# Epsilon as the bias of ScalarE's root, combiner products in quadrants and modulation rows in column tiles, in the attention stage of a two-layer adaLN kernel

## The chip, the cores and the metric

The kernel runs on one core of one Trainium2 chip. Its time is the device time of one execution, in microseconds (us); several executions give a median. Besides, one execution was recorded by the hardware profiler, and every duration and start below comes from it. The engines of the core are TensorE (PE in the profile, with PEld for its weight loads), VectorE (DVE), ScalarE (ACT) and GpSimd (POOL); SyncE (SP) issues most of the DMAs.

## The reference, cut to what matters

`x` has 4 batches of 1,024 tokens with 256 features, all in float32. There are two layers. Each takes six modulation rows per batch from a small condition, and normalises twice. Cut to layer 0, with layer 1 in a line:

```python
mod = (silu(c) @ wmod).reshape(B, 6, 1, D)          # sa, ca, ga, sb, cb, gb
ga = (2 * (ga >= 0) - 1) * maximum(abs(ga), 0.25)   # and gb
h = layernorm(x) * (1 + ca) + sa                    # (x - mean) / sqrt(var + 1e-5)
x = x + ga * linear_attention(h, queries, combiners)
h = layernorm(x) * (1 + cb) + sb
x = x + gb * experts(h)                             # 8 experts, top 2, 256 -> 1024 -> 256, relu
# layer 1: the same frame with a gated MLP that decays chunk by chunk, and 8 experts, top 2
```

The attention has no softmax. With `x` cut into slices of 64 features, it comes down to a Gram matrix of each slice over all tokens, a product of it with the combiners, and a product of that with the queries, which gives one matrix `md` per batch that all its tokens are multiplied by.

## The kernel before, in words

**Stages.** The first 104 us are the attention stage: loads, modulation rows, normalisation, attention, second normalisation, routing to experts. At its end the routed tokens are listed by expert in blocks of 128 and gathered from a table in memory, `h_rows`. Then the expert blocks run to 592 us, one after the other (`p_h`, L1610, is a block's first product, `p_y`, L1634, its second), and then layer 1, to 1073 us. The three edits of the change lie in the attention stage, with one DMA in the blocks.

**What sets the order there.** The stage is a list of pieces given to `Plan` (L47). Each piece has an engine, a cost in us, the pieces it comes after, the buffers it holds, a rank and perhaps an earliest time. `Plan.run` is a list scheduler: it plays the pieces through by their costs, lower ranks first, and emits the instructions in the order that this gives on every engine. On the chip each engine then works through its own list in that order and waits where an operand isn't there. So a changed cost or rank changes the order of instructions, not only of the piece it belongs to.

**A batch, first half** (`first_half`, L1220; `FIRSTS` holds the ranks of the four batches). `normalised` (L1085) takes groups of four chunks of 128 tokens: per chunk `bn_stats` and `bn_aggr` on DVE (L1097, L1098) into `ln_mv`; after the fourth chunk, `ln_v` = variance + epsilon (L1101); a square root on ScalarE (L1105); a Newton step for the reciprocal root on DVE, five small instructions (`newton`, L1109 to L1116); then the scaled tokens `xn` by GpSimd or ScalarE (L1126, L1128). `to_features` transposes them on TensorE (`pm_t`, L1168) and applies shift and scale on ScalarE (`h1T`, L1173); `to_tokens` transposes back (`pm_b`, L1195) and copies (L1200). TensorE takes the Gram matrices of the 64-feature slices (`pm_gram`, L1256); DVE copies them into the diagonal of a block-diagonal tile `gd` (L1267); `head_t1` (L1286) multiplies by the combiners, two products of 256 columns (`pm_t1`, shown as `pm_t` by the profile at L1289); ScalarE copies that to `t` (L1299); `pm_m` (L1311) multiplies by the queries; DVE gates it into `md` (L1324).

**A batch, second half** (`second_half`, ranks in `SECONDS`). For each pair of chunks TensorE multiplies by `md` (`pm_o`, L1352) and DVE adds to `x` (L1362). A second normalisation follows by the same `normalised`, then features again (`h2T`), the router's logits (`pm_e`, L194; `le`, L1395; `pm_l`, L1404), the choice of two experts on DVE (`route`, L420 to L446, thirteen instructions), and the way back to tokens. SP stores a group's tokens (`h_rows<-xn`, L1449, 512 KB) and, after each routing, the marks of who was chosen (`h_rows<-g_meta`, L1436). The last batch in the order, number 3, is routed in two groups (`SPLIT`).

**The handover.** When all is routed, products over the tokens give each token's place (`pm_turn`, L454 on; `g_pairs`, L466), the bounds of the first blocks (`g_limit`, L603; `g_reached`, L817), and counts (`pm_counts`, L847), from which DVE finds the row numbers of blocks 0 and 1 (L860, L869). GpSimd gathers the rows (`fetch`, L353), TensorE transposes them (`pm_x`, L1562), ScalarE copies them (L1674), and `p_h` begins.

**Modulation rows of layer 1.** Beside this, `modulation_rows` (L1512) computes layer 1's six rows: three pairs, each of four matmuls that stream 256 columns for 4 output rows (`pm_mod`, L1523), and per row one copy by ScalarE (`modulation1`, L344 on; L348 adds one to a scale row, L350 copies). They land side by side on four partitions of `half1`. In the blocks, two of them are turned into gates on DVE, and one DMA writes all to memory (L2173). Small filler products (`pm_busy`, L1033) keep TensorE running.

Of the kernel before, what the change touches and what calls it, by code (L numbers as in the profile page):

```python
# [8 lines left out]
F32 = mybir.dt.float32  # L9
F16 = mybir.dt.float16  # L10
I32 = mybir.dt.int32
AF = mybir.ActivationFunctionType
ALU = mybir.AluOpType
# [6 lines left out]
P = 128  # L20
B, S, D = 4, 1024, 256
NC = S // P
KD = D // P
# [4 lines left out]
EPS = 1e-5  # L28
# [117 lines left out]
def adaln_d2_kernel(  # L146
# [20 lines left out]
    nc = tc.nc  # L167

    const = ctx.enter_context(tc.tile_pool(name="const", bufs=1))
# [5 lines left out]
    ps_2 = ctx.enter_context(tc.tile_pool(name="ps_2", bufs=2, space=PSUM))  # L175
    ps_m = ctx.enter_context(tc.tile_pool(name="ps_m", bufs=3, space=PSUM))

    def psum(pool, shape, name):
        tag = {id(ps_1): "p1", id(ps_2): "p2", id(ps_m): "pm"}[id(pool)]
        t = pool.tile([P, 512], F32, tag=tag, name=name)  # L180
        n = 1
        for s in shape[1:]:
            n *= s
        v = t[: shape[0], :n]
        if len(shape) == 3:
            v = v.rearrange("p (a b) -> p a b", b=shape[2])
        return v
# [21 lines left out]
    rw_sb = const.tile([P, KD, STRIP], F32, name="rw_sb")  # L209
    br_sb = const.tile([P, 1], F32, name="br_sb")  # L210
    half1 = pw.tile([P, W1ROW], F32, name="half1")
    rows1 = half1[:B, : 6 * D].rearrange("p (i d) -> p i d", d=D)
    gb0 = const.tile([P, B, D], F32, name="gb0")
    poolA = tc.tile_pool(name="poolA", bufs=2)
    pa = poolA.__enter__()
    qT = pa.tile([P, KD, 4, 64], F32, name="qT", bufs=1)
    comb = pa.tile([P, KD, 4, 64], F32, name="comb", bufs=1)
# [20 lines left out]
    for b in range(B):  # L238
        for g in range(2):
            cs = slice(4 * g, 4 * g + 4)  # L240
# [21 lines left out]
    ones = const.tile([P, P], F32, name="ones")  # L262
    nc.gpsimd.memset(ones, 1.0)
    rank = const.tile([P, E], F32, name="rank")
# [50 lines left out]
    def silu_of(layer, cT):  # L315
        sT = pa.tile([P, KD, ROUTER], F32, name=f"sT{layer}", bufs=1)
        nc.vector.memset(sT, 0.0)
        nc.scalar.activation(sT[:, :, :B], cT, AF.Silu)
        return sT
# [21 lines left out]
        nc.vector.tensor_scalar(size, size, 0.25, None, ALU.max)  # L341
        nc.vector.scalar_tensor_tensor(dst, sign, -1.0, size, ALU.add, ALU.mult)

    def modulation1(pr, piece, i):  # L344

        dst, src = rows1[:, 2 * piece + i, :], pr[:, i * D : (i + 1) * D]
        if (2 * piece + i) % 3 == 1:
            nc.scalar.activation(dst, src, AF.Identity, bias=ones[:B, :1])  # L348
        else:
            nc.scalar.copy(dst, src)  # L350

# [665 lines left out]
    for k in range(KD):  # L1017
        nc.sync.dma_start(h_rows[B * S :, k * P : (k + 1) * P], ones[:1, :])
    nc.sync.dma_start(h_rows[B * S :, D:], g0.beyond[:1, :])
    sT0 = silu_of(0, c0)  # L1020
    sT1 = silu_of(1, c1)
    gate_rows = pa.tile([B, 2, D], F32, name="gate_rows", bufs=1)
# [4 lines left out]
    tiles = {}  # L1027
# [61 lines left out]
    def normalised(b, cs, key, slot, after, rank, at=0.0):  # L1089

        n = len(cs)

        def stats(c):
            if c == cs[0]:
                tiles["mv", key] = pa.tile([P, n, 2], F32, tag="ln_mv", name="ln_mv", bufs=6)
            st = pa.tile([P, 6], F32, tag="ln_st", name="ln_st", bufs=4)
            nc.vector.bn_stats(st, x_sb[:, c, b, :])  # L1097
            nc.vector.bn_aggr(tiles["mv", key][:, c - cs[0], :], st)  # L1098
            if c == cs[-1]:
                v = tiles["v", key] = pa.tile([P, n], F32, tag="ln_v", name="ln_v", bufs=6)  # L1100
                nc.vector.tensor_scalar(v, tiles["mv", key][:, :, 1], EPS, None, ALU.add)  # L1101

        def root():
            y = tiles["y", key] = pa.tile([P, n], F32, tag="ln_y", name="ln_y", bufs=6)
            nc.scalar.activation(y, tiles["v", key], AF.Sqrt)  # L1105

        def newton():
            mv, v, y = tiles["mv", key], tiles["v", key], tiles["y", key]
            nc.vector.reciprocal(y, y)  # L1109

            t = pa.tile([P, n], F32, tag="ln_t", name="ln_t")
            nc.vector.scalar_tensor_tensor(t, y, -0.5, y, ALU.mult, ALU.mult)
            nc.vector.tensor_tensor(t, t, v, ALU.mult)
            nc.vector.scalar_tensor_tensor(y, t, 1.5, y, ALU.add, ALU.mult)
            m = tiles["m", key] = pa.tile([P, n], F32, tag="ln_m", name="ln_m", bufs=6)
            nc.vector.scalar_tensor_tensor(m, mv[:, :, 0], -1.0, y, ALU.mult, ALU.mult)  # L1116

        def scaled(i):
            if ("xn", key) not in tiles:
                tiles["xn", key] = pa.tile(  # L1120
                    [P, n, D], F32, tag=slot[0], name=slot[0], bufs=plan.room[slot[0]]
                )
            dst, src = tiles["xn", key][:, i, :], x_sb[:, cs[i], b, :]
            r, m = [tiles[q, key][:, i : i + 1] for q in ("y", "m")]
            if by_gpsimd(*key, i):
                nc.gpsimd.tensor_scalar(dst, src, r, m, ALU.mult, ALU.add)  # L1126
            else:
                nc.scalar.activation(dst, src, AF.Identity, bias=m, scale=r)  # L1128

        last = []  # L1130
        for i, c in enumerate(cs):
            last = [
                plan(
                    DVE,
                    0.54 if i < n - 1 else 0.71,
                    lambda c=c: stats(c),
                    after=[*last, *after(c)],
                    rank=rank,
                    at=at,
                )  # L1140
            ]
        r = plan(ACT, 0.22, root, after=last, rank=rank - 0.2)
        d = plan(DVE, 0.9, newton, after=[r], rank=rank - 0.2)
        done = []
        for i in sorted(range(n), key=lambda i: not by_gpsimd(*key, i)):
            pool = by_gpsimd(*key, i)
            done.append(
                plan(
                    POOL if pool else ACT,
                    0.8 if pool else 0.52,  # L1150
                    lambda i=i: scaled(i),
                    after=[d, *done[:1]],
                    holds=[slot],
                    rank=rank,
                )
            )
        return done
# [57 lines left out]

    of_batch = {}

    FIRSTS, SECONDS, SPLIT = [0, 1.3, 2.42, 2.65], [1.28, 4.7, 2.66, 4.55], 3

    def first_half(b, arrival):  # L1220

# [64 lines left out]
        def head_t1():  # L1286
            p1 = tiles["p1", b] = psum(ps_1, [P, KD, 4 * 64], "pm_t1")
            for j in range(KD):
                nc.tensor.matmul(  # L1289
                    p1[:, j, :],  # L1290
                    lhsT=gd[:, j, :],
                    rhs=comb[:, j, :, :].rearrange("p a g -> p (a g)"),
                    start=True,
                    stop=True,
                )

        def head_t1_out():
            t1 = tiles["t1", b] = pa.tile([P, KD, 4, 64], F32, tag="t1", name="t1", bufs=1)
            nc.scalar.copy(t1.rearrange("p j a g -> p j (a g)"), tiles["p1", b])  # L1299

        t = plan(PE, 0.9, head_t1, after=[d], holds=[ps, t1s], rank=rank - 0.3)
        a = plan(ACT, 0.6, head_t1_out, after=[t], holds=[ps, t1s], rank=rank - 0.3)
        ps = plan.slot("p1")

# [204 lines left out]
        tiles["wm1"] = load_mod(wmod1, nc.sync)  # L1509

    loaded = plan("SP", 0.3, load_wm1, after=[weights0])
    def modulation_rows(before, pieces):  # L1512
        for piece in pieces:
            ps = plan.slot("p2")
            m = before
            for part in range(2):
                for k in range(KD):

                    def mm(piece=piece, k=k, part=part):
                        if k == 0 and part == 0:  # L1520
                            tiles["rows1", piece] = psum(ps_2, [B, 2 * D], "pm_mod")
                        at = (2 * piece + part) * D
                        nc.tensor.matmul(  # L1523
                            tiles["rows1", piece][:, part * D : (part + 1) * D],
                            lhsT=sT1[:, k, :B],
                            rhs=tiles["wm1"][:, k, at : at + D],
                            start=(k == 0),
                            stop=(k == KD - 1),
                        )

                    m = plan(PE, 0.44, mm, after=[m, loaded], holds=[ps], rank=20.0)

            for i in range(2):

                def out_(piece=piece, i=i):
                    modulation1(tiles["rows1", piece], piece, i)

                plan(ACT, 0.42, out_, after=[m], holds=[ps], rank=20.0)

    for _ in range(FILL):  # L1540
        kept_busy(0.22, [of_batch["routed"]], 35.0)
# [192 lines left out]
    plan(  # L1734
        POOL, 1.0, lambda: g0.fetch(xgbuf[1], h_rows, 1), after=[found[1]], rank=-1.5, lag=1.9
    )
    modulation_rows(m0, (0, 1, 2))
    halved = plan(DVE, 1.3, lambda: g0.with_halves(pa), after=[whole, found[1]], rank=-1.0)
    closed = plan(DVE, 2.9, lambda: g0.close_staged(pa), after=[halved], rank=-1.0)
    ps = plan.slot("p1")  # L1740
# [425 lines left out]
    def once(j):  # L2166

        if j in (4, 5):
            gate_of(rows1[:, 3 * j - 10, :], rows1[:, 3 * j - 10, :], work)
        if j == 3:  # L2170
            gate_in(1, gb0)
        if j == 5:
            nc.sync.dma_start(mod_rows1, rows1)  # L2173
        if j == 6:
            g0.weights(work)
        if 8 <= j < 8 + len(loads) - 4:
            nc.sync.dma_start(*loads[j - 8])
        if HALVES[-1] + 3 <= j < HALVES[-1] + 7:
            nc.sync.dma_start(*loads[j - HALVES[-1] - 7])
# [870 lines left out]
```

## Time and profile before

| | us |
|---|---|
| median of 5 runs | 1076.98 (1076.32 to 1078.85) |
| the profiled execution | 1074.97 |
| its span, from first to last instruction | 1073.3 |
| DVE busy, 16 to 87 us | 28.95 + 28.85 + 5.97 = 63.77 of 71 |
| ScalarE busy, 80 to 87 us | 6.92 of 7 |
| last Newton step ends | 86.71 |
| last store to `h_rows` is issued | 93.94 |
| gather of the first block's rows | 99.52 |
| first expert product (its weight load) | 104.01 |

TensorE's mean granted clock was 0.994 of full speed. In the profile's lines a group or an instruction is named by its line in the kernel, its engine, the operation, and `out<-in` with the program's names. In a timeline the columns are start and duration in us, then the instruction; in brackets stands how long the engine was idle before it, and who ended that. Neighbouring instructions of one line are merged to one row with a count. Durations of pipelined instructions overlap: the start of the next one tells what one costs.

### The profile page before, as it was taken

The numbers are of one execution on the slowest core, as the hardware profiler recorded it, in microseconds if no ns is written. First come the engines' busy times: TensorE is split into PE (matmuls) and PEld (weight loads), VectorE is DVE, ScalarE is ACT, GpSimd is POOL, SyncE is SP. The second block draws the span as 40 slices with busy tenths as digits, with TensorE's granted clock in tenths as the row PEclk, the third lists the DMA queues.
The fourth block names the chain that finished last, engine by engine and source line by source line (L and its number), as shares of the span: only waits on it lengthen the run. The fifth ranks groups of instructions, "written<-read, shape, count | busy, mean of one in ns | idle before, by whom it ended". The sixth has DMA issues, their size and how long they took to land. (4 is left out here: it accounts for less than half of the span.)

```text
span 1073.3 us, 18875 instructions
## 1 busy us (share of the span) xinstructions
PE 1039.3 (97%) x6193; PEld 803.2 (75%) x6193; DVE 601.9 (56%) x2323; ACT 395.6 (37%) x1077; POOL 424.9 (40%) x509
## 2 busy tenths in 40 slices
PE   8999999999999999999999999999999999999994
PEld 5885899989989989989999465564656567656751
DVE  7897443232222232221165588879778726698767
ACT  5766332323232323232353333423224425342521
POOL 3211466546555655554454010110106321574644
PEclk9999999999999999999999999999999999999997
DMA  8604626575553725464171211221014312352534
GB/s 283 240 21 110 216 66 209 205 275 193 180 165 104 252 63 185 137 212 148 34 267 38 75 60 59 66 83 46 19 35 136 116 61 82 100 174 77 167 104 148
DMA packets 94255, 139.81 MB, mean 130 GB/s; under 512 B 31009, under 2 KB 69933, under 8 KB 89542
## 3 DMA queue, kind: packets, MB, share of 16 engines
q0 software_dynamic: 30080, 68.89, 20.0%
q1 hardware_dynamic: 62966, 68.04, 19.6%
q10 hardware_dynamic: 1104, 1.58, 0.4%
q8 instruction: 53, 0.87, 0.3%
q14 instruction: 52, 0.43, 0.1%
HBM read 202.22 MB, written 29.17 MB: 216 GB/s over the span
## 5 line engine op out<-in xcount | busy, mean ns | idle before, releaser
L1622 ACT ACTIVATE hid<-p_h,w 128x128 f32<-128x128 f32 x504 | 143.6, 368 | 300.5 <-issue 207.5
L1634 PE MATMUL p_y<-w,hid 128*128 128x256 f32 x1008 | 230.5, 382 | 0.9 <-DMA w<-in_W,g_wrow 0.9
L2430 PE MATMUL p_u<-hT,a 128*128 128x512 f32 x512 | 229.3, 595 | 1.2 <-ACTq L2395 0.9
L1634 PEld LDWEIGHTS p_y<-w,hid 128*128 128x128 f32 x1008 | 187.2, 191 | 24.5 <-DMA w<-in_W,g_wrow 1.1
L2430 PEld LDWEIGHTS p_u<-hT,a 128*128 128x128 f32 x512 | 95.1, 190 | 102.8 <-issue 92.6
L1610 PEld LDWEIGHTS p_h<-xTq,w 128*128 128x128 f32 x1408 | 163.3, 192 | 1.7
L1610 PE MATMUL p_h<-xTq,w 128*128 128x128 f32 x1408 | 164.5, 276 | 0.0
L353 POOL DMA_INDIRECT w<-in_W,g_wrow x124 | 125.5, 1012 | 67.4 <-ACT hid L1622 42.3
L1645 DVE TENSOR_TENSOR y<-p_y,w 128x256 f32<-128x256 f32 x64 | 27.2, 424 | 193.4 <-PE p_y L1634 193.4
L914 POOL DMA_INDIRECT y<-y,g_dest x64 | 65.9, 1029 | 132.9 <-DVE y L1645 72.4
L2478 PE MATMUL p_f<-a,hf 128*128 128x256 f32 x512 | 116.9, 381 | 0.0
L2478 PEld LDWEIGHTS p_f<-a,hf 128*128 128x128 f32 x512 | 96.0, 190 | 18.5 <-issue 6.4
L2526 POOL TENSOR_TENSOR x_sb<-x_sb,step 128x256 f32<-128x256 f32 x32 | 24.5, 764 | 208.3 <-DVE step L2519 165.1
L860 DVE TENSOR_SCALAR_CACHE_REDUCE g_hits<-pm_counts,g_nth 128x128 f16<-128x128 f32 x68 | 23.6, 348 | 89.5 <-PE pm_counts L847 85.2
L1610 PE MATMUL p_h<-xT,w 128*128 128x128 f32 x608 | 71.3, 276 | 0.4 <-DVE xT L1567 0.4
L1610 PEld LDWEIGHTS p_h<-xT,w 128*128 128x128 f32 x608 | 70.3, 192 | 1.2 <-DVE xT L1567 0.6
L2442 ACT ACTIVATE hf<-p_u,decay 128x512 f32<-128x512 f32 x56 | 38.2, 684 | 78.4 <-PE p_u L2430 74.9
L2738 PE MATMUL p_e<-ew,xT 128*128 x256 | 64.9, 385 | 0.3 <-ACT y L2748 0.3
L2089 DVE TENSOR_TENSOR h<-h,mod 128x256 f32<-128x256 f32 x128 | 51.4, 423 | 4.8 <-ACT h L2079 2.7
L2446 DVE SCALAR_TENSOR_TENSOR hf<-p_u,decay,hf 128x512 f32<-128x512 f32 x56 | 41.8, 746 | 21.9 <-PE p_u L2430 10.9
L353 POOL DMA_INDIRECT xg<-ga_rows,ga_row x36 | 34.2, 949 | 45.7 <-DVE ga_row L869 16.6
L2738 PEld LDWEIGHTS p_e<-ew,xT 128*128 128x128 f32 x256 | 44.9, 191 | 8.6 <-issue 2.9
(420 smaller groups left out, 1342.0 us busy)
## 6 DMA issues: line engine op xcount, KB each, us to landing
yg<-y SPq DMA_DIRECT2D x32, 256.0 KB
xTq<-square SPq DMA_DIRECT2D x176, 32.0 KB
ew<-in_W SPq DMA_DIRECT2D x16, 288.0 KB
ga_y<-y SPq DMA_DIRECT2D x36, 128.0 KB
half<-in_W SPq DMA_DIRECT2D x16, 257.0 KB
x_sb<-in_x SPq DMA_DIRECT2D x8, 512.0 KB
h_rows<-xn SPq DMA_DIRECT2D x8, 512.0 KB
hT<-square SPq DMA_DIRECT2D x128, 32.0 KB
```

What stands on the lines that cost most here:

```text
L353: return nc.gpsimd.indirect_dma_start(out=dst, out_offset=None, in_=table, in_offset=bass.IndirectOffsetOnAxis(ap=index, axis=0), bounds_c ...
L914: nc.gpsimd.indirect_dma_start(out=table if parts == 1 else table.rearrange("r (i d) -> (r i) d", i=parts), out_offset=bass.IndirectOffset ...
L1610: nc.tensor.matmul(p1[:, i, :], lhsT=w1[:, k * H + m * P : k * H + (m + 1) * P], rhs=xT[k], start=(k == 0), stop=(k == KD - 1),)
L1622: nc.scalar.activation(hid[:, m, :], p1[:, i, :], AF.Relu, bias=w1buf[j % 2][:, KD * H + m : KD * H + m + 1],)
L1634: nc.tensor.matmul(p2, lhsT=hid[:, m, :], rhs=w2[:, m * D : (m + 1) * D], start=(m == 0), stop=(m == KH - 1),)
L1645: nc.vector.tensor_tensor(y, p2, w2buf[j % 2][:, KH * D :], ALU.add)
L2089: nc.vector.tensor_tensor(h, h, mods1[(sc, sh)[i]][:, b, :], (ALU.mult, ALU.add)[i])
L2430: nc.tensor.matmul(pu, lhsT=a[:, k, m * P : (m + 1) * P], rhs=made["n1", c, "hT"][:, k, :, :], start=(k == 0), stop=(k == KD - 1),)
L2442: nc.scalar.activation(made[key, m], made[key, m, 0], AF.Silu, scale=decays[c])
L2446: nc.vector.scalar_tensor_tensor(h, made[key, m, 1], decays[c], h, ALU.mult, ALU.mult)
L2478: nc.tensor.matmul(made[key, "p2", b], lhsT=made[key, m][:, b * P : (b + 1) * P], rhs=a1[:, m, :], start=(m == 0), stop=(m == KH - 1),)
L2738: nc.tensor.matmul(made[key, "p2"], lhsT=made[key, "xT"][:, k, :], rhs=ew_flat[:, bass.ds(made[key, "at"] + k * D, D)], start=(k == 0), st ...
```

## The change

*Epsilon.* The separate DVE instruction that adds epsilon to the variances goes. ScalarE's root reads the variances and takes epsilon from a column of constants as its bias; one instruction of the Newton step adds it on the way. *Combiner products.* Since `gd` is block-diagonal, each product of 128x128 by 256 columns is split into the two diagonal quadrants, 64x64 each. *Modulation rows.* The twelve matmuls write to partitions 0, 32 and 64 of one tile, so that three at a time use different columns of the array; the rows lie at these partitions of `half1`, and six DMAs write them to memory. *Planner.* Some costs and the ranks of the batches change.

```diff
-    rows1 = half1[:B, : 6 * D].rearrange("p (i d) -> p i d", d=D)
+    rows1 = {}
+    for i, (t, q) in {2: (0, 0), 0: (1, 0), 1: (2, 0), 5: (0, 1), 3: (1, 1), 4: (2, 1)}.items():
+        rows1[i] = (32 * t, q, half1[32 * t : 32 * t + B, q * D : (q + 1) * D])
...
+    eps = const.tile([P, 1], F32, name="eps")
+    nc.vector.memset(eps, EPS)
...
             nc.vector.bn_aggr(tiles["mv", key][:, c - cs[0], :], st)
-            if c == cs[-1]:
-                v = tiles["v", key] = pa.tile([P, n], F32, tag="ln_v", name="ln_v", bufs=6)
-                nc.vector.tensor_scalar(v, tiles["mv", key][:, :, 1], EPS, None, ALU.add)
...
-            nc.scalar.activation(y, tiles["v", key], AF.Sqrt)
+            nc.scalar.activation(y, tiles["mv", key][:, :, 1], AF.Sqrt, bias=eps)
...
-            nc.vector.tensor_tensor(t, t, v, ALU.mult)
+            nc.vector.scalar_tensor_tensor(t, mv[:, :, 1], EPS, t, ALU.add, ALU.mult)
...
-                    0.54 if i < n - 1 else 0.71,
+                    0.58,
...
-                    0.8 if pool else 0.52,
+                    0.65 if pool else 0.56,
...
-    FIRSTS, SECONDS, SPLIT = [0, 1.3, 2.42, 2.65], [1.28, 4.7, 2.66, 4.55], 3
+    FIRSTS, SECONDS, SPLIT = [0, 0.65, 1.47, 2.07], [1.45, 9.44, 5.38, 7.57], 3
...
             for j in range(KD):
-                nc.tensor.matmul(
-                    p1[:, j, :],
-                    lhsT=gd[:, j, :],
-                    rhs=comb[:, j, :, :].rearrange("p a g -> p (a g)"),
-                    start=True,
-                    stop=True,
-                )
+                for r in (slice(0, 64), slice(64, P)):
+                    nc.tensor.matmul(
+                        p1[r, j, :],
+                        lhsT=gd[r, j, r],
+                        rhs=comb[r, j, :, :].rearrange("p a g -> p (a g)"),
+                        start=True,
+                        stop=True,
+                        skip_group_check=True,
+                    )
...
-        t = plan(PE, 0.9, head_t1, after=[d], holds=[ps, t1s], rank=rank - 0.3)
+        t = plan(PE, 0.5, head_t1, after=[d], holds=[ps, t1s], rank=rank - 0.3)
...
+        for col in range(2):
+            for k in range(KD):
+
+                def mm(col=col, k=k):
+                    if k == 0 and col == 0:
+                        tiles["rows1"] = psum(ps_2, [P, 2 * D], "pm_mod")
+                    for i, (at, q, _) in rows1.items():
+                        if q == col:
+                            nc.tensor.matmul(
+                                tiles["rows1"][at : at + B, q * D : (q + 1) * D],
+                                lhsT=sT1[:, k, :B],
+                                rhs=tiles["wm1"][:, k, i * D : (i + 1) * D],
+                                start=(k == 0),
+                                stop=(k == KD - 1),
+                                skip_group_check=True,
+                            )
+
+                m = plan(PE, 0.5, mm, after=[m, loaded], holds=[ps], rank=20.0)
...
-            nc.sync.dma_start(mod_rows1, rows1)
+            for i in range(6):
+                nc.sync.dma_start(mod_rows1[:, i, :], rows1[i][2])
```

In the order that the planner now gives, the halves of the batches come in the same sequence, but their pieces interleave otherwise between 16 and 90 us. At the end of the stage, SP's last DMAs before were: store, mark, store, store, mark, mark, store; they now are: store, mark, mark, store, store, store, mark. Two of ScalarE's token copies of batch 1 stand among its last instructions of the stage. `pm_x` of block 1, which stood behind the products of block 0, now stands ahead of them, and all twelve modulation products, of which eleven did so before, and all six of their copies stand ahead of the transposes and the copy of block 0's rows; three of the products stand ahead of the counts of block 1.

## The prediction

> **What bounds the kernel now.** I read the page's busy shares first, then the 40 slices.
>
> ```profile
> PE 1039.3 (97%) x6193; PEld 803.2 (75%) x6193; DVE 601.9 (56%) x2323; ACT 395.6 (37%) x1077; POOL 424.9 (40%) x509
> ...
> DVE  7897443232222232221165588879778726698767
> ```
>
> TensorE bounds the whole, but all three parts of the change lie in the first four slices, of 27 us each, and there VectorE (DVE) is at 7, 8, 9, 7. After about 113 us the order of instructions on every engine is the same in both kernels, but for six small DMAs in place of one. So the change can only move the moment at which the first expert blocks begin; what follows is bound by TensorE and shifts with it, one for one. The table by windows shows who is late in the attention stage (start:end, length, then busy us and counts by engine):
>
> ```profile
> 16.00:48.00 32.00, 30.09 (x359) 24.93 (x357) 28.95 (x117) 24.13 (x49) 7.64 (x14) 1.00 0.72 261
> 48.00:80.00 32.00, 30.64 (x391) 26.85 (x386) 28.85 (x112) 23.28 (x47) 6.55 (x12) 1.00 0.14 42
> 80.00:87.00 7.00, 6.29 (x79) 4.85 (x81) 5.97 (x29) 6.92 (x15) 1.11 (x3) 1.00 0.48 133
> 87.00:96.00 9.00, 8.16 (x76) 4.70 (x69) 7.25 (x37) 6.17 (x14) 1.07 (x2) 1.00 0.78 174
> ```
>
> TensorE (first column) looks fuller than DVE (third), but part of it is filler products, and DVE's gaps are the 0.03 to 0.1 us between small instructions: from 16 to 87 us its waits for other engines add up to only about 1.8 us. So DVE is the bound, and ScalarE (fourth, 6.92 of 7.00) joins it from 80 to 91 us. Last, the timeline of the handover to the blocks:
>
> ```profile
> 93.94 0.45 SPq L1449 DMA_DIRECT2D h_rows<-xn  x1
> ...
> 98.27 0.16 DVE L869 SCALAR_TENSOR_TENSOR g_row<-pm_counts,g_count 128x1 int32<-128x1 f32 x1
> ...
> 99.52 1.15 POOL L353 DMA_INDIRECT xg<-h_rows,g_row  x1 [11.46 <-DVE g_blocks L626]
> ...
> 102.82 0.31 PEld L1562 LDWEIGHTS pm_x<-ident,xg 128*128 128x128 f32 x2 [0.43 <-DMA xg<-h_rows,g_row]
> ...
> 104.01 0.41 PEld L1610 LDWEIGHTS p_h<-xg,w 128*128 128x128 f32 x2
> ```
>
> The first gather of rows (99.52) needs two things: the row numbers, at 98.43, and the landing of the last 512 KB of `h_rows`, issued at 93.94. By the semaphore records that store landed at 98.48. The two are 0.05 us apart: **two co-critical chains**, and the gain is the smaller of what each gains. Call T0 the end of DVE's last Newton step (86.71). From T0 DVE does three routings without a gap, to 95.23, and the rest follows at fixed distances: row numbers T0 + 11.72, last store T0 + 11.77, first block T0 + 17.30.
>
> **Epsilon into the root.** Around one removed L1101:
>
> ```profile
> 26.94 0.18 DVE L1098 BATCH_NORM_AGGREGATE ln_mv<-ln_st 128x2 f32<-128x6 f32 x1
> 27.16 0.17 DVE L1101 TENSOR_SCALAR ln_v<-ln_mv 128x4 f32<-128x4 f32 x1
> 27.24 0.42 DVE L1097 BATCH_NORM_STATS2 ln_st<-x_sb 128x6 f32<-128x256 f32 x1
> 27.69 0.18 DVE L1098 BATCH_NORM_AGGREGATE ln_mv<-ln_st 128x2 f32<-128x6 f32 x1
> 27.79 0.40 DVE L1097 BATCH_NORM_STATS2 ln_st<-x_sb 128x6 f32<-128x256 f32 x1
> ```
>
> From aggregate to next stats it is 0.30 us with L1101 and 0.10 without: each is worth 0.20. There are 16; the first sits before statistics that wait for x (a 3.5 us DMA wait in DVE's groups), so 15 x 0.20 = **-3.0 us** on DVE before T0. L1113 becomes a scalar_tensor_tensor; such rows beside it (L1112, L1114, L1116) take 162, 176 and 168 ns against its 174: 0. The memset of one column lies in the wait for the first data: 0.
>
> ScalarE's root gets a per-partition operand as bias. The nearest row is an eviction of the modulation rows with such a bias (us in all, then ns of one):
>
> ```profile
> L348 ACT ACTIVATE half<-pm_mod,ones 4x256 f32<-4x256 f32 x2 | 0.9, 462 | 0.2 <-PE pm_mod L1523 0.2
> ```
>
> The plain copy of the same shape beside it (L350) takes 356 ns, 106 less, though the function differs too. Bounds: 0 to 0.11 each. Most of the 16 roots have slack (ScalarE is 74% busy before 80 us), but DVE waits for the last one before T0 (0.27 us at 85.75): I take **+0.1**. [...]
>
> **The planner's new order.** New piece costs and batch ranks change the interleaving from 16 to 90 us. DVE has the same work, so only its waits count. I walked the new DVE order with the durations of the rows of before. It waits for TensorE's `pm_m` before the gating `md` of batches 0 and 3 (0.35 and 0.95), for `pm_o` before four additions to x (0.6, 0.35, 0.35, 0.75), and 0.5 in smaller ones: 3.85 us in all against 1.8 before, so **+2.0**. Bounds: 0, if slack that I can't see covers them, to +3.0, at which all that L1101 frees is lost. Behind each such wait stand the statistics of other batches, for which the next root and Newton step wait. So T0 moves by -3.0 + 0.1 + 2.0 = -0.9.
>
> **The stores at the end.** Before, the 512 KB stores leave SP spread out, the last alone, 4.0 us after the one ahead. In the new order three of them stand together on SP's queue, behind the fourth of the five marks (the small stores of L1436, which wait for a routing), since ScalarE makes two copies of batch 1 only between the last ones; the last mark follows. A store issued 4 us after another landed after 4.2 us (84.96) and 4.54 (93.94); the store issued 1.58 us behind another (89.91) took 5.84. So the last lands 5.84 - 4.54 = 1.3 us later after its issue: **+1.3** on the store's chain. Bounds: 0, if the earlier two leave early enough, to +2.2, the interval between the landings of the stores issued at 88.33 and 89.91, if a whole store stands in front. The row-number chain only moves by -0.9, so the store's chain decides: -0.9 + 1.3 = +0.4.
>
> **Combiner products in quadrants.** Two products of 256 columns become four of 64x64.
>
> ```profile
> L194 PE MATMUL pm_e<-h2T,wr_sb 128*32 128x128 f32 x128 | 6.0, 282 | 0.6 <-ACT h2T L1173 0.5
> ...
> L1289 PE MATMUL pm_t<-comb,gd 128*128 128x256 f32 x16 | 4.4, 397 | 1.9 <-DVE gd L1267 1.0 <-PE pm_t L1168 0.9
> ```
>
> L1289's four records take 1.03 to 1.10 us a batch, so (1.03 - 0.38) / 3 = 0.22 a record. If diagonal quadrants run side by side, eight records take that long too: 0. One after the other: four more, 4 x 0.22 = +0.87 a batch. Gains are excluded: as many columns stream. Column tiles do run together: eight records of L194, each 0.27, end 0.43 us after the first starts. Row tiles appear nowhere in this trace. Two diagonal quadrants share neither rows nor columns, so I take the reading nearest to L194: **0**. [...] No row of before tests it.
>
> **Modulation rows.** L1523's 24 records take 4.91 + 0.60 us; in three column tiles, by L194's rate, some 4 x 0.43 = 1.7. They fill TensorE while it waits for the gather (98 to 102.82), so the saving is 0; the cover is that wait. All twelve now stand ahead of `pm_x(0)` (eleven did), three of them ahead of block 1's counts, whose gather has 2 us in hand (98.89 to 100.98); and the six copies stand ahead of ScalarE's copy of `xg`: 6 x 0.36 to 0.46 = 2.4 us from about 100, done before 103.36: 0. If the tiles ran one after the other, all 5.5 us would stand ahead of `pm_x(0)`, from about 97.9: 103.4 instead of 102.82, +0.6. One wait is new: `pm_x(1)` now stands ahead of the first block's products, and waits for the second gather (landed 103.70). With its 0.39 us the first block begins at 104.1 instead of 104.01: **+0.1**, bounds 0 and +0.4. Later it saves nothing, as TensorE waits there for DVE anyway. The six DMAs of `mod_rows1` (L2173) and the load behind them on SP come while TensorE is in the blocks: 0.
>
> **Sum:** -3.0 + 0.1 + 2.0 + 1.3 + 0 + 0.1 = +0.5 us against the profiled execution's 1074.97 (span 1073.3 and 1.67 around it): 1075.5. The median of the runs, 1076.98, lies 2.01 above the profiled one; on it: **1077.5**. A difference of 0.2% (2.15 us) is about what a measurement of this kernel can tell from no change.
>
> **Rivals.**
> - *The vector gain comes through* (0.27). The walk's waits are covered and the stores land in time: -3.0 + 0.1 + 0.1 = -2.8, so 1074.2. For it: DVE hardly waits before. Against: TensorE is 95% and ScalarE 74% busy beside it.
> - *Quadrants one after the other* (0.18). The price is 0.87 a batch on the chain `gd`, `pm_t1`, `t`, `pm_m`, `md`, and DVE stands at `md` in fixed order: 4 x 0.87 = 3.5, less 0.5 of slack in one batch, is +3.0; with the +0.5, 1080.5. It decides for slower from an L1289 group of about 1.5 us on (0.5 + 4 x 0.45 = 2.3).
> - *The stores alone make it late* (0.10). No more than 0.5 us comes off T0, and a whole store waits in front: -0.5 + 2.2 + 0.1 = +1.8, up to +2.6 if T0 keeps 0.3 more: 1078.8 to 1079.6.
> - *It does nothing that shows* (my forecast, 0.45): freed time becomes waits, and the store's landing covers the rest; own range 1075.5 to 1079.
>
> From these: faster 0.27 less a little for its weak end, 0.26; slower 0.18 and most of the 0.10, 0.27; the same 0.47. The range reaches from -3.2 (all of L1101) to +3.5: 1073.8 to 1080.5.
>
> **What would show it.** L1101 gone and DVE at T0 near 85.8; L1289 groups of about 1.05 us (1.9 if serial); more idle time of DVE at L1324 and L1362; the last `h_rows` store landing over 12.5 us after T0, and the gather waiting for it, not for `g_row`; the first block at about 104.5. I am wrong if T0 is under 84.5, or if the stores land with the row numbers.

## The result, and the profile after

The changed kernel takes 1078.98 us (median of 29 runs; before: 1077.11, 50 runs), a ratio of **1.0017, with an interval of 1.0011 to 1.0022**: 1.9 us slower, just inside the 0.2% (2.15 us) that the prediction took as the least that shows. The profiled execution took 1078.18 us (span 1076.45).

The order of things at the handover (timeline of the kernel after):

```profile
90.99 2.30 SPq L1453 DMA_DIRECT2D h_rows<-xn  x3
...
97.47 0.16 DVE L872 SCALAR_TENSOR_TENSOR g_row<-pm_counts,g_count 128x1 int32<-128x1 f32 x1
97.73 1.04 PE L1528 MATMUL pm_mod<-wmod,sT 128*4 128x256 f32 x12
...
99.25 0.61 PE L1528 MATMUL pm_mod<-wmod,sT 128*4 128x256 f32 x6 [0.47 <-ACT half L353]
99.79 1.04 PE L1038 MATMUL pm_busy<-busy 128*128 128x512 f16 x4
99.82 1.15 POOL L356 DMA_INDIRECT xg<-h_rows,g_row  x1 [13.13 <-DVE g_blocks L644]
...
102.81 0.51 PE L1572 MATMUL pm_x<-ident,xg 128*128 128x128 f32 x2 [1.99 <-DMA xg<-h_rows,g_row]
...
104.06 0.57 PE L1572 MATMUL pm_x<-ident,xg 128*128 128x128 f32 x2 [0.74 <-DMA xg<-h_rows,g_row]
```

The last Newton step now ends at 85.34 (86.71 before), and the row numbers are there at 97.63 (98.43). But three large stores leave together from 90.99, the last DMA lands at 98.78 (98.48), and the gather starts at 99.82 instead of 99.52. Then comes what is new: the modulation rows are done at 99.8, and TensorE stands still for 1.99 us, and again for 0.74. The windows of the kernel after (us; busy time of PE, PEld, DVE, ACT, POOL; then TensorE's granted clock) show what follows:

```profile
102.00:104.00 2.00, 0.51 (x2) 0.32 (x2) 1.18 (x8) 0.37 (x1) 0.22 (x1) 1.00 0.29 85
104.00:106.00 2.00, 1.94 (x10) 1.95 (x11) 0.00 (x0) 0.00 (x0) 0.00 (x0) 0.59 0.01 4
106.00:108.00 2.00, 2.00 (x12) 2.00 (x12) 0.97 (x5) 0.00 (x0) 0.00 (x0) 0.56 0.00 0
108.00:110.00 2.00, 2.00 (x20) 2.00 (x19) 1.78 (x12) 1.14 (x4) 0.00 (x0) 1.00 0.00 0
```

In the kernel before, TensorE is busy without a gap from 98 to 110 us, and the clock is 1.00:

```profile
104.00:106.00 2.00, 2.00 (x18) 1.96 (x17) 0.42 (x2) 0.60 (x2) 0.00 (x0) 1.00 0.00 0
106.00:108.00 2.00, 2.00 (x20) 2.00 (x20) 1.78 (x11) 1.14 (x4) 0.00 (x0) 1.00 0.00 0
```

From block 0's first product to block 1's it takes 10.03 us (104.43 to 114.46), before 8.70 (104.23 to 112.93). So block 1 begins 1.53 us later: 0.20 up to block 0, and 1.33 through the clock. The other 1.7 us by which this one profiled execution is longer come in its last 100 us; from layer 1's last `p_u` (L2430) to the end the traces of all kernels here take 98.4 to 100.9, without order, and I don't lay that on the change.

Of the other steps: the quadrants stand as one group (PE groups of the kernel after), and its timeline shows the four batches as 1.08, 1.18, 1.08 and 1.08 us, 8 records each, where 4 records took 1.03 to 1.13.

```profile
L1292 PE MATMUL pm_t<-comb,gd 64*64 64x256 f32 x32 | 4.4, 389 | 0.0
L1528 PE MATMUL pm_mod<-wmod,sT 128*4 128x256 f32 x24 | 2.3, 379 | 0.5 <-ACT half L353 0.5
```

DVE's waits from 30 to 97 us in the kernel after (total, times, longest):

```profile
DVE x_sb L1366 <- PE pm_o L1356: 1.3, 2, 1.1
DVE g_best L423 <- PE pm_l L1408: 0.7, 1, 0.7
DVE md L1328 <- PE pm_m L1315: 0.6, 1, 0.6
```

With another 0.7 at `md` ahead of 30 us, these are the waits for `pm_o` and `pm_m` that the prediction named, and one that it didn't: for the logits `pm_l` of the third routing.

### The profile page after: what moved, and what is told of

Same layout as the page of the kernel before. It is cut to its first block, busy times and chain, and to the rows that moved or that the text cites. A ratio compares the mean times of both kernels' runs of the same rounds, so it can differ in the third digit from the quotient of the medians.

```text
span 1076.5 us, 18889 instructions
## 1 busy us (share of the span) xinstructions
PE 1039.1 (97%) x6209; PEld 802.0 (75%) x6209; DVE 599.2 (56%) x2308; ACT 398.0 (37%) x1077; POOL 425.6 (40%) x509
```

## The experiments

Three things move from execution to execution: when the x loads let the fifth statistics begin (7.8 to 9.3 us); when the last DMA to `h_rows` lands (11.8 to 14.2 us after the last Newton step); and TensorE's clock early in the stage, which is at 0.50 for 3.4 us from 15.1 in the trace of e6, and for 6.8 us from about 14.6 in those of e5, e7, e8 and e9, but whole there in the other nine. Theory C says that the time is lost because the modulation rows no longer fill TensorE's wait and its clock drops; rival S, that the bunched stores and the hoisted transposes make the kernel late. Single traces are compared by stretches, each from its own start, and the whole by ratios to before on the same chip.

**e1, e10: filler in the gap.** In after, the two filler pieces ahead of `pm_x` get more products; no queue's order changes.

```diff
-        return plan(PE, us, lambda: busy(us), after=after, holds=[ps], rank=rank, at=at)
+        return plan(PE, us, lambda: busy(much or us), after=after, holds=[ps], rank=rank, at=at)
...
-        kept_busy(0.44, [], 40.0, at)
+        kept_busy(0.44, [], 40.0, at, 1.3 if at in (98.9, 99.4) else None)
```

> After with 12 instead of 4 filler products of 512 columns ahead of the first transposes, in the wait for the first gather; every engine's order is otherwise that of after. Theory C (clock): in after the modulation rows end 3 us sooner, TensorE stands still for 1.99 us (100.83 to 102.81) and again for 0.74, and its granted clock is 0.59 and 0.56 from 104 to 108; that costs 1.6 us between the first block's first product and its first value product (5.44 against 3.83). Then the filler brings the clock back to 1.00 there, that stretch to about 3.9, block 1's first product from 114.46 to about 112.9, and the time to 1.6 below after, about 1077.4. Rival S (stores and the hoisted transposes of block 1 alone make it late): the clock and the 1.6 are a by-product, and the time stays within 0.4 of after, about 1079.

In the profiled execution the clock is whole there. Windows of e1:

```profile
102.00:104.00 2.00, 1.17 (x6) 0.41 (x3) 1.43 (x9) 0.15 (x1) 0.94 (x1) 1.00 0.41 95
104.00:106.00 2.00, 1.22 (x11) 1.19 (x11) 0.00 (x0) 0.37 (x1) 0.00 (x0) 1.00 0.11 41
106.00:108.00 2.00, 2.00 (x20) 2.00 (x20) 1.32 (x6) 0.60 (x3) 0.00 (x0) 1.00 0.00 0
```

The stretch from block 0 to block 1 takes 8.42 us instead of 10.03: 1.6 less, as expected. The ratio is 1.0010 (0.9996 to 1.0024), which alone separates nothing.

> The kernel of e1 once more (after with 12 filler products in the wait for the gather). Theory C: the stretch from block 0's first product to block 1's near 8.4 instead of 10.0 to 10.9, ratio to before 1.0000 to 1.0008, under that of after (1.0017 and 1.0014). Rival S: 1.0015 again.

Again 8.43 us, with pauses of 1.04 and 0.72 that cost no clock; ratio 1.0006 (0.9990 to 1.0022). The two ratios lie under the two of after, but their intervals overlap; for the profiled executions the traces decide, and for the clock.

**e2: half the filler** (0.87 in place of 1.3).

> The same with 8 filler products in place of 12, so that about 1.1 us of TensorE's wait stay empty. If any pause costs clock in proportion, about 0.9 us of the 1.6 stay: 1078.2. If there is a length below which a pause costs nothing, the time is that of the full filler (1077.4, clock 1.00) or that of after (1079.0, clock near 0.57), and says on which side 1.1 us lies. By rival S: 1079 either way.

The rows came later than in after (gather at 100.31 against 99.82), so the empty stretch was 1.60 us and not 1.1. Windows of e2:

```profile
104.00:106.00 2.00, 1.43 (x7) 1.43 (x8) 0.00 (x0) 0.21 (x1) 0.00 (x0) 0.67 0.02 6
106.00:108.00 2.00, 2.00 (x11) 2.00 (x11) 0.45 (x3) 0.00 (x0) 0.00 (x0) 0.50 0.00 0
```

The stretch is 9.87 us, ratio 1.0013 (0.9999 to 1.0026). No proportion: 1.60 and 0.76 cost the whole drop, 1.04 and 0.72 (e10) nothing.

**e3, e9: the modulation rows alone.** The kernel before takes over the placement of the rows, `modulation_rows`, `modulation1` and the six DMAs, and nothing else.

```diff
+    for i, (t, q) in {2: (0, 0), 0: (1, 0), 1: (2, 0), 5: (0, 1), 3: (1, 1), 4: (2, 1)}.items():
...
-    modulation_rows(m0, (0, 1, 2))
+    modulation_rows(m0)
```

> Before with the modulation rows in column tiles alone; nothing else, old ranks and costs. Theory C: the last Newton step and the gather stay where they were (86.7, 99.5), TensorE stands still for about 2.5 us before the first transposes, the clock is near 0.57 for about 4 us, block 1 begins about 114.6 instead of 112.93, and the time is 1.6 to 2.0 above before: about 1078.9. Rival S: only the hoisted transposes count, +0.1 to +0.4: 1077.4.

> The kernel of e3 once more (before with the modulation rows in column tiles alone), because its 4.8 us over before are three times what its traced stretch explains (9.87 against 8.70 from block 0's first product to block 1's). Theory C with a pause of 2 to 3 us: ratio 1.0015 to 1.003, the stretch 9.8 to 10.9. If it is 1.0045 again, the pause costs elsewhere too, and that stays open.

Ratios 1.0045 (1.0029 to 1.0060, 6 runs) and 1.0036 (1.0023 to 1.0049, 12 runs): **this edit alone is slower than the whole change**. Pauses of 2.84 and 2.67 us, stretches of 9.87 and 11.33. Windows of e9:

```profile
106.00:108.00 2.00, 0.71 (x3) 0.51 (x4) 0.57 (x4) 0.37 (x1) 0.00 (x0) 0.75 0.25 68
108.00:110.00 2.00, 2.00 (x10) 2.00 (x11) 0.00 (x0) 0.00 (x0) 0.00 (x0) 0.50 0.00 0
110.00:112.00 2.00, 2.00 (x11) 2.00 (x10) 1.10 (x5) 0.00 (x0) 0.00 (x0) 0.50 0.00 0
112.00:114.00 2.00, 2.00 (x13) 2.00 (x12) 1.66 (x11) 1.14 (x4) 0.00 (x0) 0.55 0.00 0
```

Here the clock stays low for 6.8 us, in after for 3.4. The traces explain 1.2 to 2.6 us by the clock, and 0.4 by the hoisted transposes (gather to block 0: 4.71 and 4.77, in e4, e7 and e11 without the hoist 4.33 to 4.38; before itself has 4.70, as a modulation product stands there ahead of `pm_x` when the rows come). That is 1.6 to 3.0 of the 3.9 and 4.8 measured; the ends of the intervals (2.5 and 3.1) are near its upper end. What is left, if anything, these two traces don't show; the last paragraph of this section comes back to it.

**e6: the same with filler behind it** (11 products in place of 2).

> Before with the modulation rows in column tiles (as e3, which was 0.45% slower) and 11 filler products in place of 2 behind them, so that TensorE stands still for under 1 us. Theory C: clock 1.00, block 1's first product 8.4 to 8.7 us after block 0's instead of 9.87, ratio to before 1.001 to 1.002 where e3 had 1.0045. Rival M: the tiles cost by another way (six DMAs in the blocks, the hoisted transposes), then the clock is whole and the ratio still above 1.003.

Ratio **1.0006** (0.9995 to 1.0017), an interval that doesn't meet those of e3 and e9. Windows of e6:

```profile
104.00:106.00 2.00, 2.00 (x11) 1.11 (x10) 1.76 (x12) 1.54 (x4) 0.03 (x1) 1.00 0.27 78
106.00:108.00 2.00, 1.78 (x16) 1.59 (x15) 0.61 (x4) 0.37 (x1) 0.00 (x0) 1.00 0.00 0
```

The stretch is 8.80, a little over the 8.4 to 8.7 expected. My filler was clumsy: its other piece stands ahead of `pm_counts`, DVE waits 2.4 us there, and the row numbers come 13.65 us after the last Newton step instead of 11.70. Even so, nearly all of the loss is gone. It was the empty time, not the tiles.

**e4: after with the modulation rows of before** (in one strip on four partitions, one DMA).

```diff
-    modulation_rows(m0)
+    modulation_rows(m0, (0, 1, 2))
```

> After with the modulation rows of before (24 records in a row), so that their 5.5 us fill the wait again; epsilon, quadrants and planner numbers as in after. Theory C: clock 1.00 throughout; last Newton step near 85.3 and gather near 99.8 as in after; the hoist of block 1's transposes is gone too; block 1 begins near 113.1 and the time is +0.2 on before: 1077.3. Rival S: bunched stores still stand there, so the time stays near 1078.6.

Ratio 1.0003 (0.9990 to 1.0015), clock 1.00 with one pause of 0.92 us. The stretch is 9.24 us and not 8.70: a filler of 0.60 us and a longer wait for `pm_x` (0.73 against 0.41) stand in it. The last Newton step is 73.6 us after the seventh statistics begin (after 73.7; before 75.3, e3 74.9). Epsilon, quadrants and the new order together come out even.

**e5: after once more.**

> After itself once more, beside the other three on one chip. In the runs so far the landing of the x loads moved by 1.5 us from execution to execution, and the stores by 1.4, so stretches are read from their own start. Theory C: last Newton step 73.7 us after the seventh pair of statistics begins (before: 75.1 in two traces), first product of block 1 about 10.0 us after that of block 0 (before 8.70), clock near 0.57 between them; time +1.9 on before. Rival S: the 10.0 was an accident of one execution and goes back to 8.7.

Ratio 1.0014 (1.0003 to 1.0026); a pause of 2.77 us, 6.8 us at clock 0.50, a stretch of 10.86. So the 10.03 was no accident. The 73.7 was not met (76.3). The clock was low early as well:

```profile
14.60:21.40 6.80, 6.80 (x26) 4.48 (x26) 5.12 (x23) 1.94 (x5) 1.09 (x2) 0.50 0.99 306
```

There DVE waits 0.56 us for `pm_modT` and 0.69 for `pm_mod`, and the tenth and eleventh statistics are 4.5 us apart, as they are 3.8 to 5.2 us apart in the five traces with this early drop and 3.31 in all nine without. In e9 it is the same: 77.1 us against the 74.9 of e3. So I lay the 76.3 on the clock, though no run tests that alone. The change is not behind it, as after and e3, the same kernels as e5 and e9, don't have this drop. Ahead of it TensorE waits 1.4 to 2.1 us for an `xn` of GpSimd (0.81 in before, 0.88 in after; 1.40 in e3, without a drop).

**e8: the stores spread, and filler.**

```diff
-            back = to_tokens(key, slot, hT2, held2, f, rank + 0.1)
+            back = to_tokens(key, slot, hT2, held2, f, rank + 0.1 if b != 1 else 7.0)
...
+        ps = plan.slot("p1")
+        plan(PE, 0.05, lambda: busy(2.7), after=[m], holds=[ps], rank=19.9)
```

> After with the copies to tokens of batch 1 ranked ahead, so that its last 512 KB store leaves before the fourth mark instead of among the last three, and with 12 filler products behind the modulation rows. If the bunched stores cost what the traces show (landing 13.8 to 14.0 us after the last Newton step against 13.1 with the order of before on one chip, 13.4 against 11.8 on another), the last landing comes back to within 0.5 of the row numbers, and with the clock whole the time is 1 to 2 us below before. If the landing stays at 13.8, it is the DMA rings and not the order, and the time is that of before.

The last DMA lands 11.8 us after the last Newton step, where e5, after on the same chip, has 14.2, and e6 and e7 there, with the order of before, 12.8 and 13.0. So against e8 the bunching costs 2.4 us, and against the order of before 1.2 to 1.4. But the ratio is 1.0009 (0.9993 to 1.0026), since other things got later. DVE's waits in e8, from 30 us:

```profile
DVE g_best L423 <- PE pm_l L1408: 2.0, 1, 2.0
DVE x_sb L1366 <- PE pm_o L1356: 1.4, 2, 1.1
DVE ln_y L1111 <- ACT ln_y L1107: 1.4, 1, 1.4
```

The row numbers now come 13.10 us after the Newton step, and they decide: of two co-critical chains one was moved forward, and the other back.

**e7: epsilon alone,** in the order of before.

```diff
-            nc.scalar.activation(y, tiles["v", key], AF.Sqrt)
+            nc.scalar.activation(y, tiles["mv", key][:, :, 1], AF.Sqrt, bias=eps)
...
-            nc.vector.tensor_tensor(t, t, v, ALU.mult)
+            nc.vector.scalar_tensor_tensor(t, mv[:, :, 1], EPS, t, ALU.add, ALU.mult)
```

> Before with epsilon in the root alone, planner costs and ranks of before, so that every queue keeps its order. By the prediction's first term DVE frees 15 x 0.20 = 3.0 us up to the last Newton step, and what it gives back shows as new waits; with the old order I expect waits of 1 to 2 us (75.1 becomes 73 to 74), the last store 7.2 us after the Newton step as before, no pause of TensorE over 1 us, and a time 1 to 2 us below before. Rival: the freed time comes back as waits whole, and the time is that of before.

Ratio 0.9985 (0.9968 to 1.0001); the medians are 1078.77 and 1078.81, so the whole alone shows no gain. The trace shows one in its stretch. From the 17th statistics to the last Newton step it takes 61.0 us; four traces with the same order and without the edit (before, e3, e6, e9) take 62.6 to 63.0. Twelve L1101 lie in this stretch, 12 x 0.20 = 2.4; 1.5 to 1.9 arrive. DVE's waits for ScalarE's root rise there from 0.6 to 1.3.

**e11: epsilon and quadrants,** order and modulation rows of before: the edits of e7, and

```diff
-                    p1[:, j, :],
-                    lhsT=gd[:, j, :],
+                        p1[r, j, :],
+                        lhsT=gd[r, j, r],
```

> Before with epsilon in the root and the combiner products in quadrants, planner costs and ranks of before, modulation rows of before. The quadrants run side by side in after (8 records in 1.08 us against 4 in 1.03 to 1.13), so they should add nothing to epsilon alone (0.9985): 0.998 to 0.999, the groups of L1289 near 1.08. Rival: they cost 0.87 a batch when nothing in the order covers them, then the ratio is above 1.000.

Ratio **0.9982 (0.9970 to 0.9994)**, 1076.80 against 1078.80 us: faster than before, and the only kernel here whose whole interval is. The groups take 1.08 to 1.34 us: side by side in this order too. The stretch between the blocks is 8.70, its pause 0.85.

**e12: all three edits, planner numbers of before, filler as in e6.**

> All three edits with the planner costs and ranks of before, and 11 filler products in place of 2 behind the modulation rows. If the planner's new order is what eats the vector gain (bunched stores, the wait for the third routing's logits), this is faster than after with filler: 0.9985 (epsilon) plus 0.0006 (tiles with filler), so about 0.999. If the order is neutral, it is that of e1: 1.001.

Ratio 1.0005 (0.9993 to 1.0018). It has the fault of e6: 2.4 us of DVE waiting for counts behind my filler, row numbers 13.62 us after the Newton step. So it doesn't tell whether the new order is worse than the old one; that stays open.

**The clock over all executions.** TensorE's mean granted clock was measured in every execution, not only in the profiled one. Averaged over a kernel's executions, with before on the same chip in brackets, it is 0.9903 (0.9930) in e3, 0.9904 (0.9933) in e9, 0.9919 (0.9935) in e5, 0.9920 (0.9930) in e1, 0.9924 (0.9933) in e10, 0.9927 (0.9935) in e6 and 0.9931 (0.9930) in e4; each difference is uncertain by 0.0005 to 0.0009. As an estimate, 0.001 of 1,077 us is 1.1 us of full speed lost. So the modulation rows alone lose some 2.9 and 3.1 us by the clock, and with 0.4 for the hoist 3.3 and 3.5 of the 4.8 and 3.9 measured, which lies in both intervals. With filler behind them some 0.9 is left (e6), with the rows of before nothing (e4). In e1 and e10 about 1.0 is left too, though their traces show none at the handover: their filler seems to have covered the wait in some executions only. These means hold every low stretch, the early one too (e7 has 0.9919, with the modulation rows of before), so they bear theory C out, but can't divide the loss by place.

## Why the prediction was right or wrong, point by point

The forecast was "no difference that shows", at +0.5 us; measured were +1.9, within the range and nearly at the edge of what shows. That the verdict held is in part luck: the steps that I summed gave +0.2 at block 0, and the clock, which the sum didn't have, +1.3. The step that failed is the price of a saved filler.

- **Epsilon, -3.0 less new waits.** Right in kind. On the first chip the last Newton step moved by -1.38 (-1.6 from the seventh statistics on) where -0.9 stood; e7 shows 1.5 to 1.9 of the 2.4 in its stretch. From 16 us to that step DVE's waits of over 0.25 us went from 1.3 (the prediction has about 1.8) to 3.0, so the new ones are 1.7 and not 2.0; nearly all lie where named, at `pm_o` and `pm_m`.
- **The root's bias, +0.1.** L1107 takes 298 ns in the median where L1105 took 206: +0.09, under the 0.11 of the row used.
- **The stores, +1.3 on their chain.** Right in the profiled pair, and the main reason why the vector gain is lost: the landing moved from 11.77 to 13.44 us after the Newton step, +1.67, inside the bounds of 0 to 2.2, and the gather waited for it and not for the row numbers. That chain moved too, by 0.58 for `pm_l`, which I had not seen; it was covered. But the two chains only 0.05 us apart were an accident of that one execution of before: in the six other traces with its order of stores the last one lands 12.8 to 13.1 us after the Newton step, and where no filler holds the row numbers up (11.7) the store decides by over 1 us. On like chips the new order lands 0.6 to 1.4 later.
- **Quadrants, 0.** Right, and now shown: e11 and every trace with them (eight records in 1.08 to 1.34 us). The four records of before took 1.03 to 1.13 us, not to 1.10 as the prediction has it. One after the other, eight would have taken some 1.9 us, as an estimate from the 1.03 of four and 0.22 for each one more. The measurement decides: two row tiles that write different partitions of one tile in PSUM did run at once here.
- **Modulation rows, 0 ("the cover is that wait").** Wrong. I priced the shorter work at nothing because it lay in a wait, and did not ask what the wait looks like when it is empty. L1523 was itself what kept TensorE busy in it. The term should have been +1.3 in the profiled execution (1.6 against the same kernel with filler), and up to 2.4 where the clock stays low for 6.8 us (e5). Its rows are the windows from 104 to 108 us: clock 1.00 before, 0.59 and 0.56 after.
- **Hoisted transposes, +0.1.** From gather to block 0 after takes 4.61 us and before 4.70, so the 0.20 at block 0 is the gather's 0.30 and nothing of the hoist. Where no modulation product is in the way, it costs up to 0.4 (e3 and e9 against e4, e7 and e11), the upper bound.
- **The rivals.** Quadrants in series: excluded. The stores alone: real, but not enough to make it slower by more than the rest gave back (e4: 1.0003); its upper end doesn't add up, as 0.3 more on T0 makes +2.1 and not +2.6. That the gain comes through: only without the other two parts (e11).

Without the failed term the profiled steps give 0.20 at block 0; with it 1.53 at block 1. The profile alone could have shown it: a line that names what fills the 4.9 us, and the question what stands there when it shrinks to 2.3.

## What to carry to other kernels

Work that lies in a wait is free to keep, but not always free to remove: if it is what keeps TensorE busy, shorten it only with something in its place, and read the clock column of the windows behind it (here 0.50 for 3.4 to 6.8 us). A gain of one engine must be followed to every chain that meets at the next common wait; here the row numbers gained 0.8 us and the stores gave it all back. And try the parts of a change alone: one part (e9) cost more than the whole, and two others (e11) gained 0.18%.

## What the runs showed of the hardware

At the handover the low clock lasts 3.4 us, or twice that. A quarter microsecond at a time, it goes to 0.50 at 104.4 in after and comes back at 107.75:

```profile
104.25:104.50 0.25, 0.25 (x3) 0.25 (x3) 0.00 (x0) 0.00 (x0) 0.00 (x0) 0.71 0.12 33
...
107.75:108.00 0.25, 0.25 (x4) 0.25 (x4) 0.25 (x2) 0.00 (x0) 0.00 (x0) 0.96 0.00 0
```

That is 3.4 us; e2 and e3 have the same length, e5 and e9 6.8 us, twice as much, after pauses of 2.77 and 2.67. In these five traces the drop comes 2.8 to 3.6 us after the pause begins, when TensorE has taken up work again.

How busy TensorE is in the 3.41 us ahead of a drop can be counted. Here are those in after, busy for 24%, and in e10 3.41 us that hold its two pauses but for the first 0.2 us, busy for 54%, or 48% with that 0.2 in it, which no drop follows:

```profile
100.95:104.36 3.41, 0.81 (x4) 0.62 (x5) 2.11 (x13) 1.38 (x4) 0.96 (x2) 1.00 0.28 78
102.79:106.20 3.41, 1.83 (x13) 1.65 (x14) 0.55 (x3) 0.37 (x1) 0.17 (x1) 1.00 0.19 56
```

Summed from windows of a quarter and half a microsecond, the 3.41 us ahead of the drop are busy for 15% in e3, 19% in e5, 22% in e9 and 31% in e2. No drop follows in after, late in layer 1, where TensorE stands still once for 1.59 us, from 1022.48, and is busy for 53% of the 3.41 us that begin there:

```profile
1022.48:1025.89 3.41, 1.82 (x11) 1.68 (x12) 0.37 (x2) 0.73 (x3) 0.81 (x1) 1.00 0.47 131
```

So in these cases it is the busy share of such a stretch that orders them, 15 to 31% with a drop and 48 and 53% without, and not the length of one pause: 1.60 and 0.76 close together were enough, and 1.04 and 0.72 were not, nor was 1.59 alone. The shares rest on the modelled ends of the matmuls in the profile. What happens between 31 and 48%, and why the low clock lasts 3.4 us in some traces and 6.8 in others, no run here tells.
